# Two graph attention layers on one core: another order of the preparation, row blocks of features in pairs, and layer 1's groups ending without sums

## The chip, the core and the metric

The kernel runs on one core of one Trainium2 chip. The core has five engines with queues of their own: TensorE for matrix products and transposes (the profile shows its matmuls as PE and its weight loads as PEld), VectorE (DVE), ScalarE (ACT), GpSimd (POOL), and SyncE (SP), which here issues nearly all DMA transfers. Each queue is worked off in the order in which it was written; engines wait for each other through semaphores. The metric is device time in microseconds. The kernel before took 5032.46 us, the median of three runs (5031.23 to 5033.24).

## What is computed

Everything is float32. There are 4096 nodes with 512 features; `adj` is 4096 x 4096. Each layer normalises its input, clips it at zero and adds what an attention with 8 heads of 64 features makes of it:

```python
h = max(layernorm(x), 0)
# layer 0
d = h @ W.T + b                             # 4096 x (8 heads x 64)
e = src[:, None] + trg[None, :]             # for each head, from d
e = where(e >= 0, e, 0.01 * e) + adj
x = x + softmax(e) @ d
# layer 1
h = max(layernorm(x), 0)
a = (h Wq)(h Wk)^T / 8 - 1e16 * (1 - max(adj, eye))
x = x + sum over heads of softmax(a) @ (h Wv) @ Wo
```

The division by the sum of a softmax row can be made anywhere between its exponentials and `Wo`, since it is one factor for each row and head.

## The kernel before

A block is 128 rows (32 of them, `NB`). Heads go in pairs `c`; a **group** is one pair for one block. The program has five stretches.

**Preparation** (lines 419 to 446 call it). It takes the input in 8 turns `q` of four blocks. `load_rows` brings 1 MB of `x` into one of three buffers. `moments` has VectorE take means and variances (`bn_stats` at line 320, `bn_aggr` at 321) and ScalarE the root (line 323). `normed` inverts the root and has GpSimd write the normed rows `hn` (line 336). `turned_rows` transposes them on TensorE (`htp`, line 348), ScalarE clips them on the way out of PSUM (`hT`, line 351), and 1 MB of `hT` is stored (line 354). `halves` multiplies them with a small matrix that holds the source and target projections (`lp`, line 363); VectorE takes the result out as `lr` (line 368), and four small stores write the target halves to `trg_d` (line 370). After every second turn `load_targets` (line 128) loads 1024 columns of two heads' target halves back, spread over all partitions. `sources` transposes the source halves (`sp`, line 377), and `first_features` makes the first pair's features (`mp`, 32 matmul instructions at line 387, taken out by an add at line 393). The work of a turn is spread over five loop passes, so that pass `q` does the moments of turn `q`, the norm of `q - 1`, the transposes of `q - 2`, the halves of `q - 3`, and sources and features of `q - 4`. The tiles `htp`, `lp` and `mp` share three PSUM buffers.

**Layer 0, three pairs of heads** (lines 447 to 486): for each group ScalarE makes the logits (`leaky`, line 147), VectorE adds `adj` and takes the row extreme (`masked`, line 158), ScalarE takes exponentials (line 168), TensorE transposes (line 181) and multiplies with the features (line 203). `sources_by_sets` runs once, early in this stretch. **Layer 0's last pair together with layer 1's projections** follows (lines 735 to 780); the change doesn't touch it.

**Layer 1** (lines 1003 to 1060) has 512 sets, each 32 rows of a pair; four sets are a group, 128 groups in all. One pass `s` of the loop does, in this order on the queues: transposes of set `s - 4` on VectorE (line 936) and TensorE (line 942), the row extreme of an earlier pair of sets (`smallest`, `nmB`, line 913), one step of an ended group (`finish`), the scores of set `s` (line 878) and their masking by VectorE (line 894), the exponentials of set `s - 3` on ScalarE (line 929), and the product of set `s - 8` with the values (line 959). The mask comes from `adj` in pair 0 (GpSimd writes it at line 865) and from DRAM afterwards. `finish` copies the group's result out of PSUM (`oT`, line 969), adds the four sets' sums on TensorE (`den`, line 972), inverts them on VectorE (line 976), transposes the result in the next pass (`back`, line 979), multiplies (line 981) and stores 64 KB to `att_d` (line 985), which is laid out by rows.

**Output** (lines 1063 to 1084) starts when the loop is over: `wot` is loaded, then for each of 32 blocks `xt` and `at` are loaded, `at` is transposed (`atr`, line 1075), copied by ScalarE (line 1077), multiplied with `wot` (`oo`, 8 matmul instructions, line 1080), added (line 1083) and stored.

Of the kernel before, what the change touches and what calls it, by code (L numbers as in the profile page):

```python
# [15 lines left out]
P = 128  # L16
# [7 lines left out]
def kernel(  # L24
# [74 lines left out]
    with tc.tile_pool(name="a0k", bufs=1) as pk, tc.tile_pool(name="a0v", bufs=4) as pv, tc.tile_pool(  # L99
# [216 lines left out]
        def moments(R):  # L316
            R.mv = psb.tile([P, XR, 2], F32, name="mv")
            for r in range(XR):
                stats = psb.tile([P, 6], F32, name="stats")
                nc.vector.bn_stats(stats, R.x[:, r])  # L320
                nc.vector.bn_aggr(R.mv[:, r], stats)
            R.rstd = psb.tile([P, XR, 1], F32, name="rstd")
# [17 lines left out]
        def turned_rows(R, q):  # L340
# [3 lines left out]
            for j in range(XR // 2):  # L344
# [9 lines left out]
            nc.sync.dma_start(  # L354
                hT_d[bass.ts(q, XR)].rearrange("r p k -> p r k"), R.hT.rearrange("p r k n -> p r (k n)")
            )
# [25 lines left out]
        def first_features(R, q):  # L382

            tp = ptr.tile([P, TW], F32, tag="tr", name="mp")
            for r in range(XR):
                for kc in range(KC):
                    nc.tensor.matmul(
                        tp[:, bass.ts(r, PR)], lhsT=R.hT[:, r, kc, :], rhs=wt[:, kc, :PR],
                        start=(kc == 0), stop=(kc == KC - 1),
                    )  # L390
            if q % 2 == 0:
                feats[0].append(pv.tile([P, 2 * XR, PR], F32, tag="v", name="v"))
            nc.vector.tensor_add(
                feats[0][-1][:, bass.ts(q % 2, XR), :], tp[:, : XR * PR].rearrange("p (r d) -> p r d", r=XR),
                bb[:, :PR].unsqueeze(1).to_broadcast([P, XR, PR]),
            )

# [21 lines left out]
        with tc.manual_schedule():  # L419
# [6 lines left out]
            for q in range(NQ + 5):  # L426
                if q + 2 < NQ:
                    rows.append(load_rows(q + 2))
                if q < NQ:
                    moments(rows[q])  # L430
                if 0 <= q - 1 < NQ:
                    normed(rows[q - 1])
# [3 lines left out]
                if 0 <= q - 2 < NQ:  # L436
                    turned_rows(rows[q - 2], q - 2)
# [6 lines left out]
                if 0 <= n - 1 < NQ:  # L444
                    sources(rows[n - 1], n - 1)
                    first_features(rows[n - 1], n - 1)
# [4 lines left out]
            for s in range(total + 6):  # L451
                G, h = step(s) if s < total else (None, 0)
                for half in range(2):
# [8 lines left out]
                    if (s, half) == (1, 0):  # L462
# [9 lines left out]
                    if s < total:  # L472
                        masked(G, h, half)
                    for e in endings:
# [307 lines left out]
    att_d = dram.tile([N, HD], F32, name="att_d")  # L782
    pen_d = dram.tile([N // 32, P, N // 4], F32, name="pen_d")

# [9 lines left out]
    NT = (QK_ - VC) // P  # L794
    with tc.tile_pool(name="a1t", bufs=1) as pt, tc.tile_pool(name="a1k", bufs=4) as pkk, tc.tile_pool(
        name="a1v", bufs=GS
    ) as pv, tc.tile_pool(name="a1a", bufs=6) as pa, tc.tile_pool(name="a1q", bufs=2) as pq, tc.tile_pool(
        name="a1x", bufs=1
    ) as px, tc.tile_pool(name="a1s", bufs=6) as psb, tc.tile_pool(
# [313 lines left out]
```

## Time and profile before

| what | value |
|---|---|
| median of the runs | 5032.46 us |
| the profiled execution's own time | 5033.3 us, with a span of 5031.5 us |
| mean granted TensorE clock | 0.978 |
| busy, PE / DVE / ACT / POOL | 4802.4 / 4530.7 / 3929.0 / 362.1 us |
| weight loads, PEld | 3552.2 us |
| first `masked` of layer 0 starts | 110.62 us |
| scores of layer 1 from which the chain holds hardly anything but TensorE | 2588.67 us |
| last scores of layer 1 start | 4861.42 us |
| first transposes of the output | 4893.63 us |
| last matmul of the output ends | 5027.69 us |

The span is the time from the first to the last instruction of one profiled execution. A busy time is the sum of an engine's instruction times; matmuls overlap, so that a fully busy PE is not yet PE at its best. In the chain of waits each piece is the time until the next link could start, and "xN" counts instructions, two for each float32 matmul. A releaser is the event after which an idle engine went on.

### The profile page before, as it was taken

The page shows a single profiled execution, that of the slowest core. Times are in us where ns is not written, and L with a number is a line of the kernel's source. Part 1 is how long each engine was busy: PE and PEld are TensorE (multiplying, and loading weights), DVE is VectorE, ACT ScalarE, POOL GpSimd, SP SyncE. Part 2 cuts the span into 40 slices and gives each one's busy share as a digit, 9 for nine tenths or more (in the row PEclk, how much of TensorE's full clock was granted, in tenths as well). Part 3 has the DMA queues.
Part 4 walks back from the last instruction along what each step waited for, and adds up shares of the span by engine and source line. Part 5 has one row for each costly group of instructions (what it writes and reads, how often), then busy time and mean ns, then how long its engine had stood idle before and what let it go on. Part 6 is the DMA issues. An engine that isn't in the chain of part 4 may idle for free.

```text
span 5031.5 us, 147684 instructions
## 1 busy us (share of the span) xinstructions
PE 4802.4 (95%) x62810; PEld 3552.2 (71%) x62810; DVE 4530.7 (90%) x8205; ACT 3929.0 (78%) x4581; POOL 362.1 (7%) x648
## 2 busy tenths in 40 slices
PE   6999999999999869999989999999999999999999
PEld 5888888888888757677746666666666666666654
DVE  4999999999999898888579999999999999999971
ACT  3999999999999898888568888666666666666651
POOL 1000000000000011111112222000000000000000
PEclk8999999999999979999999999999999999999999
DMA  6444454445444474444387777433353434444425
GB/s 217 152 163 146 163 194 163 147 161 195 163 147 161 129 167 134 141 140 138 98 240 240 237 239 246 145 124 126 126 160 122 127 127 143 141 127 127 127 98 176
DMA packets 339908, 794.35 MB, mean 158 GB/s; under 512 B 57520, under 2 KB 168368, under 8 KB 314160
## 3 DMA queue, kind: packets, MB, share of 16 engines
q1 hardware_dynamic: 338720, 783.86, 48.7%
q8 instruction: 493, 8.08, 0.7%
q14 instruction: 167, 1.37, 0.1%
q10 hardware_dynamic: 528, 1.05, 0.1%
HBM read 652.48 MB, written 132.25 MB: 156 GB/s over the span
## 4 chain that ended last, share of the span: by engine, by line
PE 46%; DMA 1%; ACT 1%; issue 1%; DVE 1%; SPq 0%; POOL 0%; ACTq 0%; DVEq 0%; POOLq 0%
PE o L959 18%; PE sc L878 18%; PE tr L942 6%; PE oo L1080 2%; DMA a<-in_adj_dram 1%; ACT t L929 1%; PE nmB L913 1%; PE den L972 0%; DVE t L936 0%; PE back L979 0%; SPq L852 0%; PE mp L697 0%; DVE t L894 0%; ACT aT L1077 0%; PE mpv L709 0%
## 5 line engine op out<-in xcount | busy, mean ns | idle before, releaser
L894 DVE CUSTOM_DVE_ANT_0 t<-sc,a 128x512 f32<-128x512 f32 x2048 | 1291.1, 686 | 78.2 <-issue 56.3
L929 ACT ACTIVATE t<-t,nm 128x1024 f32<-128x1024 f32 x1024 | 1168.4, 1143 | 167.6 <-DVE nm L918 167.6
L959 PEld LDWEIGHTS o<-t,v 128*64 128x64 f32 x16384 | 883.9, 137 | 423.2 <-issue 339.7
L878 PE MATMUL sc<-k,q 64*32 64x512 f32 x16384 | 1002.5, 597 | 8.9 <-DVE nm L894 8.9
L959 PE MATMUL o<-t,v 128*64 128x128 f32 x16384 | 1007.0, 276 | 0.2 <-ACT oT L969 0.2
L936 DVE STREAM_TRANSPOSE t<-t 128x1536 f32<-128x1536 f32 x512 | 908.1, 1774 | 8.9 <-ACT t L929 5.9
L158 DVE CUSTOM_DVE_ANT_0 t<-t,a 128x2048 f32<-128x2048 f32 x384 | 876.1, 2282 | 28.7 <-ACT t L147 23.6
L181 PE MATMUL tr<-ident,t 128*128 128x128 f32 x6144 | 781.7, 278 | 38.1 <-ACT pT L190 20.0
L181 PEld LDWEIGHTS tr<-ident,t 128*128 128x128 f32 x6144 | 665.4, 141 | 130.6 <-issue 65.5
L203 PE MATMUL o<-pT,v 128*64 128x128 f32 x12288 | 756.8, 276 | 0.8 <-DVE pT L192 0.8
L147 ACT ACTIVATE t<-tb,src 128x4096 f32<-128x4096 f32 x192 | 732.0, 3813 | 13.7 <-DMA tb<-trg_d 13.7
L168 ACT ACTIVATE t<-t,nm 128x4096 f32<-128x4096 f32 x192 | 731.7, 3811 | 6.9 <-DVE nm L163 6.6
L203 PEld LDWEIGHTS o<-pT,v 128*64 128x64 f32 x12288 | 664.1, 137 | 60.7 <-issue 46.9
L948 ACT COPY t<-tr 128x512 f32<-128x512 f32 x512 | 298.9, 584 | 480.2 <-PE tr L942 477.4
L192 DVE COPY pT<-tr 128x1024 f32<-128x1024 f32 x549 | 652.7, 1214 | 9.8 <-PE tr L181 9.8
L878 PEld LDWEIGHTS sc<-k,q 64*32 64x32 f32 x16384 | 251.0, 106 | 340.7 <-issue 298.5
L942 PE MATMUL tr<-ident,t 128*128 128x128 f32 x2048 | 342.6, 287 | 11.5 <-ACT t L929 9.5
L569 ACT ACTIVATE lk<-tb,srcb 128x1024 f32<-128x1024 f32 x256 | 282.3, 1113 | 83.5 <-DVE nm L579 76.4
L579 DVE CUSTOM_DVE_ANT_0 bt<-lk,ba 128x1024 f32<-128x1024 f32 x256 | 301.9, 1215 | 25.6 <-ACT e L703 12.7
L618 DVE STREAM_TRANSPOSE bt<-bt 128x2048 f32<-128x2048 f32 x128 | 295.1, 2306 | 29.0 <-ACT bt L611 29.0
L942 PEld LDWEIGHTS tr<-ident,t 128*128 128x128 f32 x2048 | 213.7, 140 | 111.3 <-issue 85.0
L611 ACT ACTIVATE bt<-bt,nm 128x1024 f32<-128x1024 f32 x256 | 290.3, 1135 | 0.4 <-DVE nm L600 0.3
(116 smaller groups left out, 3961.4 us busy)
## 6 DMA issues: line engine op xcount, KB each, us to landing
a<-in_adj_dram SPq DMA_DIRECT2D x192, 1024.0 KB
a<-pen_d SPq DMA_DIRECT2D x384, 512.0 KB
ba<-in_adj_dram SPq DMA_DIRECT2D x512, 128.0 KB
a<-in_adj_dram SPq DMA_DIRECT2D x512, 128.0 KB
pen_d<-a SPq DMA_DIRECT2D x128, 512.0 KB
h<-hT_d SPq DMA_DIRECT2D x96, 256.0 KB
qk_d<-e SPq DMA_DIRECT2D x64, 256.0 KB
x<-in_x_dram SPq DMA_DIRECT2D x8, 1024.0 KB
```

Source lines behind the costliest of these rows:

```text
L147: nc.scalar.activation(t, targets[G.c, h], AF.Prelu, bias=src[:, G.g, 2 * G.c + h : 2 * G.c + h + 1], alpha=SLOPE)
L158: nc.vector.tensor_tensor_reduce(out=t, in0=t, in1=rows_of_adj[G, f], scale=-1.0, scalar=FMAX, op0=ALU.add, op1=ALU.min, accum_out=nm[:, f ...
L168: nc.scalar.activation(G.t[h], G.t[h], AF.Exp, bias=G.nm[h][:, NCH : NCH + 1], scale=-1.0, accum_out=G.sm[:, h : h + 1],)
L181: nc.tensor.transpose(tr[:, bass.ts(b % 4 * 2 + h, P)], G.t[h][:, bass.ts(i * MB + b, P)], ident)
L192: nc.vector.tensor_copy(pT, tr)
L203: nc.tensor.matmul(G.o[h * D : (h + 1) * D, :P], lhsT=feats[G.c][i][:, b, bass.ts(h, D)], rhs=pT[:, bass.ts(b % 4 * 2 + h, P)], start=(mb ...
L878: nc.tensor.matmul(sc[h][bass.ts(a, SQ), :], lhsT=G.q[bass.ts(h, D), bass.ds(G.q0 + k * SQ, SQ)], rhs=keys[G.c][half][bass.ts(h, D), a, :] ...
L894: nc.vector.tensor_tensor_reduce(out=t[:, G.ring + k, h, cols], in0=scs[half][h], in1=a[:, cols], scale=1.0, scalar=FMAX, op0=ALU.add, op1 ...
L929: nc.scalar.activation(u, u, AF.Exp, bias=G.nm[k // 2][:, k % 2, h : h + 1], scale=-1.0, accum_out=G.sm[:, k, h : h + 1],)
L936: nc.vector.transpose(u, u)
L942: nc.tensor.transpose(tr[:, bass.ts(h * NT + m, P)], t[:, G.ring + k, h, bass.ds(VC + m * P, P)], ident)
L959: nc.tensor.matmul(G.o[bass.ts(h, D), :P], lhsT=v[:, b, bass.ts(h, D)], rhs=t[:, bass.ds(G.ring, GS), h, bass.ds(at, SQ)], start=(mb == 0) ...
```

## The change

It has three parts.

1. **Preparation.** The root is split off `moments` as `deviations` and written after the transposes' copies of an earlier turn; transposes and norm stand ahead of the moments in a pass. Features are made for two blocks a pass instead of four (`first_features(q, j)`, 16 matmul instructions), their add is written at the start of the next pass (`first_features_out`), and the store of `hT` goes after a turn's second add. What is not made when the passes end (7 of 16 halves) is made in the first two sets of passes of layer 0's first group, beside its first logits. `sources_by_sets` moves from `(1, 0)` to `(3, 1)`.
2. **Layer 1's groups.** `finish` only copies the result out and stores it, still transposed and not divided, to `att_d`, which is now laid out by pair. The sums of all sets stay in one tile, `sums`. Once 16 groups of a pair are done, `divided` adds the sums with one matmul (`tot`), inverts, transposes (`invT`), writes the factors to `inv_d`, loads four pieces of `att_d` with their factors, multiplies them (GpSimd; VectorE for the last half) and stores them back.
3. **Output.** It runs inside layer 1's loop in the passes after the last scores (`projected`, one block a pass, ten in all), and after it for the other 22 blocks, from chunks of two blocks (`load_chunk`). `at` comes transposed already, so no transposes and no copies are left. The ninth chunk's load first runs whatever is left of the divisions.

```diff
-            for q in range(NQ + 5):
+            for q in range(NQ + 4):
                 if q + 2 < NQ:
                     rows.append(load_rows(q + 2))
+                some_out()
+                if 0 <= q - 2 < NQ:
+                    turned_rows(rows[q - 2], q - 2)
+                if 0 <= q - 1 < NQ:
+                    normed(rows[q - 1])
                 if q < NQ:
                     moments(rows[q])
-                if 0 <= q - 1 < NQ:
-                    normed(rows[q - 1])
+                    deviations(rows[q])
                 if q == 1:
                     prepared(wn, col)
                     turned_weights(wn)
-                if 0 <= q - 2 < NQ:
-                    turned_rows(rows[q - 2], q - 2)
...
                 if 0 <= n - 1 < NQ:
                     sources(rows[n - 1], n - 1)
-                    first_features(rows[n - 1], n - 1)
+                some_features(q - 2)
+            some_out()
...
+                    if s < 3:
+                        some_features(NQ)
+                        some_features(NQ)
...
         def finish(G):
             oT = px.tile([P, P], F32, name="oT")
             nc.scalar.copy(oT, G.o[:, :P])
-            den = pm.tile([P, 512], F32, tag="ms", name="den")
...
+            nc.sync.dma_start(att_d[G.c, :, bass.ts(G.g, P)], oT)
+
+        def inverted(c, half):
+            tot = pm.tile([P, 512], F32, tag="ms", name="tot")
+            nc.tensor.matmul(
+                tot[:, : 2 * SG * GS], lhsT=bands,
+                rhs=sums[:, c, half].rearrange("p h g k -> p (h g k)"), start=True, stop=True,
+            )
+            inv = px.tile([P, P], F32, tag="oT", name="inv")
+            nc.vector.reciprocal(inv[:SQ], tot[:SQ, : 2 * SG * GS])
+            yield
+            invT = pm.tile([P, 512], F32, tag="ms", name="invT")
+            nc.tensor.transpose(invT[:, :SQ], inv[:SQ], ident[:SQ, :SQ])
+            rows = px.tile([P, SQ], F32, name="rows")
+            nc.scalar.copy(rows, invT[:, :SQ])
+            for h in range(2):
+                nc.sync.dma_start(
+                    inv_d[c, h, bass.ts(half, SG * P)].rearrange("(q i) -> q i", i=SQ), rows[bass.ts(h, D)]
+                )
+            yield
+
+        def scaled(c, half):
+            last = (c, half) == (HC - 1, 1)
+            zs = []
+            for i in range(4):
+                cols = bass.ts(half * 4 + i, 4 * P)
+                z = pz.tile([P, 2, 4 * P], F32, tag="z", name="z")
+                nc.sync.dma_start(z[:, 0], att_d[c, :, cols])
+                for h in range(2):
+                    nc.sync.dma_start(z[bass.ts(h, D), 1], inv_d[c, h, cols].partition_broadcast(D))
+                yield
+                zs.append((cols, z))
+                if i % 2 == 0:
+                    continue
+                yield
+                for cols, z in zs:
+                    (nc.vector if last else nc.gpsimd).tensor_mul(z[:, 0], z[:, 0], z[:, 1])
+                yield
+                for cols, z in zs:
+                    nc.sync.dma_start(att_d[c, :, cols], z[:, 0])
+                zs = []
...
+        def load_chunk():
+            i = len(chunks)
+            if i >= NG // 2 // ZR:
+                for d in divisions:
+                    for _ in d:
+                        pass
+                divisions.clear()
+            if i < NB // ZR:
+                at = pat.tile([P, HC, ZR * P], F32, name="at")
+                nc.sync.dma_start(at, att_d[:, :, bass.ts(i, ZR * P)].rearrange("c p n -> p c n"))
+                xt = pa.tile([P, ZR, DM], F32, tag="a", name="xt")
+                nc.sync.dma_start(xt, x1_d[bass.ts(i, ZR * P), :].rearrange("(r p) d -> p r d", p=P))
+                chunks.append((at, xt))
+
+        def projected(j):
...
+            nc.vector.tensor_add(xt[:, r], xt[:, r], o)
+            if r == ZR - 1:
+                nc.sync.dma_start(out[bass.ts(i, ZR * P), :].rearrange("(r p) d -> p r d", p=P), xt)
+                load_chunk()
...
+                if n > 1 and n % (SG * GS) == 1:
+                    divisions.append(divided(*divmod(n // (SG * GS) - 1, 2)))
+                for d in divisions[:1]:
+                    if next(d, d) is d:
+                        divisions.pop(0)
...
-        for rb in range(NB):
-            xt = pw.tile([P, DM], F32, name="xt")
...
+            for j in range(rb, NB):
+                projected(j)
```

## The prediction

> **What bounds the kernel now.** I first read the busy time by stretch (columns: stretch; total; busy time and instructions of PE, PEld, DVE, ACT, POOL; granted clock; DMA share; GB/s), because the 95% that the page gives PE is an average over stretches with different limits.
>
> ```profile
> 50.00:100.00 50.00, 43.20 (x469) 40.47 (x468) 16.93 (x50) 10.24 (x13) 12.06 (x16) 0.89 0.65 227
> 2900.00:2950.00 50.00, 49.77 (x792) 30.75 (x784) 49.31 (x122) 41.40 (x67) 11.76 (x16) 1.00 0.75 242
> 3300.00:4000.00 700.00, 700.00 (x11056) 437.84 (x11062) 670.86 (x1551) 461.63 (x815) 18.66 (x78) 1.00 0.42 132
> 4900.00:4950.00 50.00, 49.66 (x150) 24.08 (x149) 8.25 (x12) 6.44 (x12) 0.00 (x0) 0.99 0.58 185
> ```
>
> Preparation (first row) has no full engine, so a loop of waits bounds it. In layer 1 (second row pair 0, third row later pairs) TensorE is full, with VectorE close behind: 98.6% in pair 0, 95.8% later. In the output (last row) TensorE works alone. The timeline of one preparation turn (start, length, what, idle before and its releaser) shows the loop:
>
> ```profile
> 61.80 0.69 DVE L393 TENSOR_TENSOR v<-mp,bb 128x512 f32<-128x512 f32 x1 [6.11 <-PE mp L387]
> ...
> 65.60 0.14 DVE L326 RECIPROCAL rstd<-rstd 128x4 f32<-128x4 f32 x1
> 65.78 0.30 ACT L323 ACTIVATE rstd<-mv,eps 128x4 f32<-128x4 f32 x1 [8.63 <-DVE rstd L326]
> ...
> 65.99 1.92 ACT L351 ACTIVATE hT<-htp 128x1024 f32<-128x1024 f32 x2
> ...
> 67.04 5.46 PE L387 MATMUL mp<-wt,hT 128*128 128x128 f32 x32 [2.27 <-ACT hT L351]
> ```
>
> The add waits for the features; behind it VectorE's moments wait; ScalarE's root waits for them and its copies `hT` stand behind the root; the features wait for a PSUM buffer that the copies free. Once round is 10.75 us (this add at 61.80, the next at 72.55). The chain of waits (start, length, link) gives one group of layer 1, then the output:
>
> ```profile
> 4757.56 0.17 PE den L972 x8
> 4757.73 1.88 PE sc L878 x32
> 4759.61 1.90 PE o L959 x32
> 4761.50 0.59 PE tr L942 x4
> 4762.09 0.14 PE nmB L913 x2
> 4762.23 0.14 PE back L979
> ...
> 4887.35 6.14 DMA at<-att_d
> ...
> 4895.39 6.29 PE oo L1080 x8
> ...
> 4999.10 0.59 ACT aT L1077
> 4999.69 0.04 issue
> 4999.73 7.13 PE oo L1080 x16
> ```
>
> In the group every link is TensorE, end to end: taking one out moves everything up. In the output two blocks take 7.13 us of matmuls out of 8.08 (4999.73 to 5007.82); the rest is transposes and the copy.
>
> **Preparation: -19 us.** The new order cuts the loop: the copies `hT` no longer stand behind the root, the add no longer waits for matmuls written just before it. What a pass then costs each engine, by the durations of the old loop: PE `htp` 1.91, `lp` 1.08, `sp` 0.33, half the features 1.9 to 2.7 (32 took 3.74 to 5.46), some 0.5 of issue gaps: about 6.0 us. DVE four times 0.66 + 0.18, plus 0.30 for root and shift, 0.35 `lr`, 0.18 `src`, an estimated 0.4 for half an add: 4.6. ACT 2.2, POOL 3.0. So TensorE bounds, at 6.0. The first logit halves start at 34.15 now and about 34.5 after (the start, up to 30 us, is the same small matrix products and copies). Six turns of 6.0, the last pass shorter, put the eighth at about 73.5; it starts at 96.27 now. That is 22.8 saved, and the first `masked` at 110.62 hangs on it by the same steps (target stores, their reload, `leaky`, `adj`). Against it: on SP's queue the fourth `hT` store now stands between the last reload and the first `adj` tile, 1 MB more to move, 2.6 us at the 400 GB/s that DMA reaches at best here. Three more `hT` stores stand ahead of the fourth `adj` tile, which waits for VectorE anyway and is needed some 16 us later. The seven late feature halves fill a TensorE that idles there (its first long run of transposes starts at 128.00), so they are free; without that cover they cost 7 x 1.9. Their adds are 7 x 0.4 = 2.8 on VectorE, part of it inside its waits for ScalarE (2.6 and 1.95 us there): 1.2. The moved `sources_by_sets` made VectorE wait 1.38 before and may again: nothing. Ends: -27 (warm clock, 5.5 a pass, nothing given back) and -10 (a pass moves 2 MB; at 290 GB/s that is 7.2 us, not 6.0).
>
> **Layer 1: -35 us.** `den` and `back` leave the chain: 0.17 + 0.14 = 0.31 a group; 125 of the 128 groups end before the tail begins: 38.8. VectorE loses 0.275 + 0.131 a group; of an 18.04 us group it is busy 17.29 in later pairs, so 16.88 against TensorE's new 17.73, and in pair 0 17.8 - 0.4 = 17.4. TensorE stays the bound; in pair 0 with 0.3 to spare. The result copy stays on ScalarE, and the store behind it on SP stands ahead of a mask load that is five sets early. What is added: seven divisions inside the loop. `tot` and `invT` are not in the trace; by the nearest rows (`nmB` 0.14 for two matmuls, a transpose 0.15) about 0.3. The inverse on VectorE waits for `tot`, which stands behind TensorE's last product of that pass, and the next `squares` wait behind the inverse: up to 0.5 late. I take 0.6 in all, 4.2 for seven; ends 0.3 and 1.7. The transfers of a division (3 MB over some ten passes) have room at 132 GB/s.
>
> The 28 multiplications on GpSimd have no row of their own. Two-input rows there are 240 ns for 32 columns and 458 for 128; carried on to 512 columns that is an estimated 1.34 us, two in a row. Behind them waits only the next `parted`, needed two sets later. One rule speaks against this: the Trainium skill, *GPSIMD Engine Reference*, Key points, says that GpSimd shares its SBUF interfaces with VectorE, so that the two get in each other's way when VectorE runs a two-port mode or reads two SBUF tensors. If a pair held VectorE up for its whole 2.7 us, the slack of 0.85 a group would hide a third, and 14 pairs would cost about 26 us. The rows say otherwise: with GpSimd busy 11.76 of 50 us in pair 0, line 894 took 683 ns, and 687 in later pairs without it; line 936 took 1778 and 1773. GpSimd's work there has one input, so the two-input case is not quite shown. I take nothing, and 13 for the range.
>
> **Output: -17 us.** From 4865.20, where the last regular transposes start, the span runs 166.3 us. After: TensorE has 8 x 1.90 of products, 4 x 0.59 of transposes and 0.14: 17.7; 32 blocks of 3.57 (7.13 / 2): 114.2; 0.4 for the last division. The ten interleaved blocks fill the waits for ScalarE that this tail has now, so these add up end to end: 132.3. Behind the last matmul, as now, an add and a store: 3.8, and 0.7 for a store twice as large. That would be 136.8, 29.5 less than now.
>
> But the ninth chunk waits for the last half's division, and that is a chain through DRAM. It is started from SP only behind the store of block 11: add and store issue, 1.1. Then: load two pieces with factors (1 MB in six issues; the reload of 1 MB of targets took 4.3 from issue at 102.00 to `leaky` at 106.29: 5.0 with four issues more), two multiplications on VectorE at 0.69 (line 1083), store (the last one took 3.1 to the end of the span), load again 5.0 because there are two buffers, multiply 1.4, store 3.1, load chunk 4.0: 24.1 in all. TensorE has blocks 12 to 15 meanwhile, 14.3 (four PSUM buffers, so no add holds them up). So it stands still for about 10, and starts again at a low clock: eight instructions took 6.29 after the 6 us wait of now, 3.57 otherwise, 2.7 more. 29.5 - 12.7 = 17. Ends: -29 (the chain is covered) and -5 (each of the loads takes the 6.14 us of the output's first one and the chunk behind queues too).
>
> **Sum.** -19 - 35 - 17 = -71 from the span of 5031.5: 4960.5. The profiled execution reported 5033.3 and the median of the runs is 5032.46, 1 us above the span, so 4962.
>
> **Rivals.** *No stall in the output* (0.17): the division's transfers are short enough or start early enough. For it: 256 KB pieces with DMA engines 58% busy; against it: five steps, each waiting for the one before. 4949. *Preparation bounded by transfers or SP* (0.12): 2 MB a pass, and SP's reloads wait for the small stores to land (10.2 us in six waits now, the longest 5.8). It gives -8 instead of -19: 4973. *VectorE takes over in layer 1* (0.10): pair 0 is at 98.6% and GpSimd's pairs collide: half the gain is lost, 4980. *Slower than before* (0.03): the division chain costs far more. Its place is the ninth chunk, its price per step; without it the change is worth 84, so it decides from 84 + 14.3 for five DMA steps, about 20 us a step. The longest single wait for a load in the output is 6.14 us, so I hardly believe it; at 22 us a step it would be 5044. That the change doesn't do what it says I exclude: with the order of instructions at hand, `den`, `back` and `atr` are gone.
>
> **How the numbers follow.** The forecast case has 0.55, its own range 4948 to 4976. The range 4942 to 4985 takes in all but the slower case and the far ends of the unknown costs. A change under 0.2% (10 us) can't be told from none here. All cases but the last are over it: faster 0.95, same 0.02, slower 0.03.
>
> **What would show it.** Preparation: adds of features 6 us apart instead of 10.75, first logits near 80 instead of 106.29. Layer 1: group period 17.73 instead of 18.04, lines for `tot` eight times, line 894's mean still near 687 in windows with multiplications. Output: no transposes, one hole of 10 us in TensorE at block 16, fed by a DMA. I am wrong if adds stay 8 us or more apart, if VectorE's idle in layer 1 vanishes, or if the hole is missing or longer than 20.

## The result, and the profile after

The changed kernel takes 4974.47 us (median of 4 runs, 4972.49 to 4976.71), beside 5032.85 us (5031.23 to 5037.03) for the kernel before in the same comparison. The ratio is 0.9883, with a 95% interval of 0.9866 to 0.9900. The profiled span went from 5031.5 to 4973.0 us, so 58.5 us are to be found, where the prediction had 71.

Where they came from can be read by the starts of the same instructions in both traces. VectorE's 32x32 transposes of layer 1 (`squares`) are good marks: four a group, 512 in all.

| stretch, by its marks | before | after | change | predicted |
|---|---|---|---|---|
| start to the first `squares` of layer 1 | 2566.30 | 2551.35 | -14.9 | -19 |
| pair 0, first two groups | 35.25 | 37.69 | +2.4 | -0.6 |
| pair 0, the other 30 groups | 548.76 | 547.22 | -1.5 | -8.7 |
| pairs 1 to 3, 95 groups | 1714.74 | 1688.71 | -26.0 | -25.9 |
| from there to the end of the span | 166.45 | 148.03 | -18.4 | -17 |

The last column splits the prediction's -35 for layer 1: 0.31 us a group, less 0.6 for each division, one of them in pair 0 and six later. The rows of pairs 1 to 3 and of the end are right within 1.5 us. The misses are pair 0 (both of its rows) and, less so, the preparation.

The busy time by stretch of the changed kernel (columns: stretch; total; busy time and instructions of PE, PEld, DVE, ACT, POOL; granted clock; DMA share; GB/s):

```profile
50.00:100.00 50.00, 30.64 (x321) 28.38 (x320) 13.21 (x33) 14.24 (x10) 6.03 (x8) 0.80 0.74 260
2900.00:2950.00 50.00, 49.66 (x760) 30.30 (x744) 49.04 (x115) 42.49 (x70) 15.35 (x20) 1.00 0.91 288
3300.00:4000.00 700.00, 699.97 (x10888) 437.25 (x10889) 673.08 (x1499) 468.04 (x830) 28.90 (x87) 1.00 0.43 143
4880.00:4930.00 50.00, 40.01 (x87) 17.36 (x86) 9.45 (x15) 0.00 (x0) 0.00 (x0) 0.86 0.71 229
```

In the second row, pair 0, VectorE is still busy for 49.04 of 50 us (before 49.31), although two of its operations a group are gone. A busy share that hardly falls when work is removed is the sign to look there. The last row shows a hole in TensorE in the output, 10 us in 50, and a granted clock of 0.86 with it.

A group of a later pair in the chain of waits (start, length, link) is the old one without `den` and `back`:

```profile
4741.61 1.88 PE sc L915 x32
4743.49 1.90 PE o L996 x32
4745.39 0.58 PE tr L979 x4
4745.97 1.88 PE sc L915 x32
...
4759.20 0.14 PE nmB L950 x2
4759.34 1.88 PE sc L915 x32
```

From 4741.61 to 4759.34 are 17.73 us, the predicted period; before it was 18.05. The output's end in the same view:

```profile
4889.30 4.70 DMA z<-inv_d
...
4894.12 0.70 DVE z L1044
...
4894.85 1.99 DMA att_d<-z
...
4899.59 4.12 DMA z<-inv_d
...
4904.93 5.34 DMA at<-att_d
...
4910.40 58.01 PE oo L1079 x128
```

The last half's division runs through DRAM link by link and hands over to TensorE at 4910.40, 23.7 us after the products of block 11 ended (4886.69), which the last store ahead of it waited for.

The timeline of VectorE in the preparation (start, length, what, idle before and its releaser):

```profile
45.06 0.42 DVE L396 TENSOR_TENSOR v<-mp,bb 128x256 f32<-128x256 f32 x1
...
49.42 0.42 DVE L396 TENSOR_TENSOR v<-mp,bb 128x256 f32<-128x256 f32 x1
...
55.92 0.69 DVE L320 BATCH_NORM_STATS2 stats<-x 128x6 f32<-128x512 f32 x1 [5.79 <-DMA x<-in_x_dram]
...
59.67 0.42 DVE L396 TENSOR_TENSOR v<-mp,bb 128x256 f32<-128x256 f32 x1
```

The adds come 4.4 to 5.3 us apart here (35.34, 39.81, 45.06 and 49.42: 4.7 on the mean), better than the 6 predicted, and then once 10.25 us apart: VectorE waits for the last rows.

### The profile page after: what moved, and what is told of

Same layout as the page of the kernel before. It is cut to its first block, busy times and chain, and to the rows that moved or that the text cites. A ratio compares the mean times of both kernels' runs of the same rounds, so it can differ in the third digit from the quotient of the medians.

```text
span 4973.0 us, 145263 instructions
## 1 busy us (share of the span) xinstructions
PE 4747.3 (95%) x61554; PEld 3507.7 (71%) x61554; DVE 4509.1 (91%) x7969; ACT 3912.2 (79%) x4557; POOL 396.1 (8%) x676
## 4 chain that ended last, share of the span: by engine, by line
PE 42%; DMA 3%; issue 2%; SPq 1%; ACT 1%; DVE 1%; POOL 0%; ACTq 0%; POOLq 0%; DVEq 0%
PE sc L915 17%; PE o L996 17%; PE tr L979 5%; PE oo L1079 2%; DMA a<-in_adj_dram 2%; ACT t L966 1%; PE nmB L950 1%; SPq L889 1%; POOL a L902 0%; DVE t L931 0%; PE mp L727 0%; DMA z<-inv_d 0%; PE mpv L739 0%; DMA att_d<-z 0%; DMA v<-v_d 0%
## 5 line engine op out<-in xcount | busy, mean ns | idle before, releaser
L973 DVE STREAM_TRANSPOSE t<-t 128x1536 f32<-128x1536 f32 x512 | 907.7, 1773 | 5.0 <-ACT t L966 2.0
L979 PE MATMUL tr<-ident,t 128*128 128x128 f32 x2048 | 348.5, 288 | 11.6 <-ACT t L966 8.4
```

What stands on the lines that cost most here:

```text
L973: nc.vector.transpose(u, u)
L979: nc.tensor.transpose(tr[:, bass.ts(h * NT + m, P)], t[:, G.ring + k, h, bass.ds(VC + m * P, P)], ident)
```

## The experiments

The runs were timed in other comparisons than the result, in which the kernel before had medians of 5032.50 to 5033.90. Differences of two or three us between medians are no more than this spread; where a gain is that small, the marks of the profiled runs carry the reading.

### Pair 0: what holds 18.3 us a group

The periods of single groups, from start to start of every fourth `squares`, were steady in pair 0: 18.35 us before and 18.31 after (medians over 22 groups). The prediction had used 18.04 for both. The timeline of all engines of the changed kernel shows one set of four (weight loads, reads of accumulators and the small operations left out):

```profile
2970.24 1.15 ACT L966 ACTIVATE t<-t,nm 128x1024 f32<-128x1024 f32 x1 [1.26 <-DVE nm L955]
...
2972.52 1.04 ACT L901 ACTIVATE a<-a 128x1024 f32<-128x1024 f32 x1
...
2972.89 1.78 DVE L973 STREAM_TRANSPOSE t<-t 128x1536 f32<-128x1536 f32 x1
...
2973.64 1.04 POOL L902 TENSOR_SCALAR a<-a 128x1024 f32<-128x1024 f32 x1 [4.41 <-ACT a L901]
...
2974.72 0.69 DVE L931 CUSTOM_DVE_ANT_0 t<-sc,a 128x512 f32<-128x512 f32 x1
```

The masked logits start 1.83 us after `squares`, 0.04 us after GpSimd's mask is done (2973.64 + 1.04). Where nothing is waited for, a following operation starts 1.70 us after. The mask depends on ScalarE's relu, which stands behind ScalarE's exponentials, which wait for VectorE's minimum (the first line): a loop of some 18.3 us a group. The theory made from this: before, VectorE's own work filled the period and the mask lay just under it; the change took instructions of 0.41 us out of that work, and the mask's wait took their place. Four runs test it.

**Masks two sets ahead, in the changed kernel:**

```diff
+            with_self(*step(1), pens[1])
+            made_penalty(*step(1), pens[1])
...
-                if s + 1 < total:
-                    with_self(*step(s + 1), pens[s + 1])
+                if s + 2 < total:
+                    with_self(*step(s + 2), pens[s + 2])
...
-                if s + 1 < total:
-                    made_penalty(*step(s + 1), pens[s + 1])
+                if s + 2 < total:
+                    made_penalty(*step(s + 2), pens[s + 2])
```

> The changed kernel, with pair 0's mask tiles made two sets ahead instead of one (the diagonal on VectorE, the relu on ScalarE and the scaling on GpSimd all one set earlier); nothing is left out. Theory 1 (the mask chain took up what the change freed): in pair 0 VectorE's own work is now 18.0 us a group (two times 4.45 + 4.55), the other 0.32 is the wait of the plain sets for GpSimd's tile; it goes, the period falls from 18.32 to 18.0 and 32 groups give 10 us: about 4964. Rival (VectorE is simply full at 18.3, its busy share is 98%): the period stays at 18.3 and the time at 4974. Rival 2 (TensorE would have bound at 17.73 but for the mask): 32 x 0.59 = 19 us, 4955.

Measured: 4972.68 us (4972.26 to 4976.67), by its range not to be told from the changed kernel; the profiled span is 1.9 less. The period is what the theory said, and the time isn't. The median group takes 18.00 us, and the wait is gone:

```profile
2966.03 1.78 DVE L973 STREAM_TRANSPOSE t<-t 128x1536 f32<-128x1536 f32 x1
...
2966.77 1.05 POOL L902 TENSOR_SCALAR a<-a 128x1024 f32<-128x1024 f32 x1 [4.10 <-DMA a<-in_adj_dram]
...
2967.73 0.65 DVE L931 CUSTOM_DVE_ANT_0 t<-sc,a 128x512 f32<-128x512 f32 x1
```

1.70 us from `squares` to masked logits. (The mask beside them is that of a later set.) Over the last 30 groups of pair 0 this gives 5.1 us (547.22 to 542.12) and not 9: one group at a division rose to 20.36 us, because the mask now needs its adj tile a set sooner and SP issues that tile behind the division's loads. And 5 us are lost where layer 1 begins, since two masks must be made before the first logits: the first `squares` come 3.6 us later, and the first eight sets take 1.3 us more. So the wait is shown, and with it the cost of an edit that moves work of a start-up.

**The same edit in the kernel before:**

> The kernel before, with the same edit: pair 0's masks made two sets ahead. Theory 1 (before, VectorE's own work of 4.45 + 4.55 + 4.60 + 4.75 = 18.35 us a group set the period, and the mask chain lay just under it): no gain, 5032 within 3, period 18.35. Rival (the mask chain set the period of pair 0 before as well): 10 us faster, 5022, period 18.0.

Measured: 5035.26 us against 5033.39, ratio 1.0002 (0.9993 to 1.0011). The median period fell by 0.09 us, from 18.35 to 18.26, against 0.31 in the changed kernel. So before, the mask was close behind but VectorE's own work set the pace, as the theory has it. The rows of both runs without the mask's wait (this run, then the changed kernel's) show how a full VectorE looks here: 98.6% busy, the rest in gaps too short to have a releaser.

```profile
2750.00:2850.00 100.00, 100.00 (x1564) 61.51 (x1562) 98.61 (x242) 84.27 (x139) 25.44 (x33) 1.00 0.74 237
```

```profile
2750.00:2850.00 100.00, 100.00 (x1539) 61.49 (x1545) 98.55 (x235) 85.33 (x140) 25.81 (x34) 1.00 0.74 238
```

Between these two runs the change is worth 18.26 - 18.00 = 0.26 us a group, not 0.41, although the two instructions that it removed lasted 0.41.

**The diagonal off VectorE as well.** GpSimd multiplies the finished corner of the mask by one minus the identity:

```diff
-                nc.vector.tensor_max(diag, diag, ident[bass.ts(b, SQ), bass.ts(b, SQ)])
+                nc.gpsimd.tensor_mul(diag, diag, other[bass.ts(b, SQ), bass.ts(b, SQ)])
...
                 nc.gpsimd.tensor_scalar(a, a, -1.0, -BIG, ALU.add, ALU.mult)
+                with_self(G, k, a)
```

> The changed kernel with the masks two sets ahead and the diagonal taken from VectorE (0.18 us and some 0.03 beside it, four times a group): GpSimd multiplies the finished 32x32 corner by one minus the identity. Same result, nothing left out. Theory 1: VectorE's work in pair 0 falls to about 17.2 us a group, TensorE's 17.73 becomes the bound there too: 32 x 0.59 = 19 us under the changed kernel, about 4955, period 17.7 to 17.8. Rival (GpSimd's two-input work beside VectorE's two-input work slows VectorE, or the longer mask chain binds again): period 18.0 or more, 4964 or more.

One part of the computation is changed here, other than the expectation says: adj holds weights up to 1e9 and not only zeros and ones, and a node's own edge loses its weight. The instructions are those intended. Measured: 4963.05 us (4961.15 to 4966.00), median period 17.73 us, and for the 30 groups 534.35 us, 12.9 less than the changed kernel. The period is the theory's, the time 8 us more: the first `squares` come 4.0 us sooner, but the first eight sets take 44.8 us instead of 37.7. TensorE fills the stretch, and VectorE has room for the first time:

```profile
2800.00:2900.00 100.00, 99.98 (x1553) 62.62 (x1557) 96.21 (x213) 86.77 (x141) 34.67 (x58) 1.00 0.75 240
```

The rival's slowdown isn't there. The groups of VectorE and GpSimd in 200 us of pair 0 (busy, mean ns; idle before):

```profile
L934 DVE CUSTOM_DVE_ANT_0 t<-sc,a 128x512 f32<-128x512 f32 x180 | 113.5, 686 | 7.2 <-issue 3.9 <-POOL a L899 0.2 <-POOL a L904 0.2
L899 POOL TENSOR_TENSOR a<-a,other 32x32 f32<-32x32 f32 x45 | 11.0, 245 | 3.8
L1047 POOL TENSOR_TENSOR z<-z 128x512 f32<-128x512 f32 x2 | 2.5, 1290 | 0.1
```

GpSimd now runs a two-input operation in each set, and VectorE's masked logits, which take `sc` from PSUM and only the mask from SBUF, still take 686 ns.

**The diagonal as a sum ahead of the relu,** with only the first mask made before the loop:

```diff
-                nc.vector.tensor_max(diag, diag, ident[bass.ts(b, SQ), bass.ts(b, SQ)])
+                nc.gpsimd.tensor_add(diag, diag, ident[bass.ts(b, SQ), bass.ts(b, SQ)])
...
-                nc.scalar.activation(a, a, AF.Relu)
-                nc.gpsimd.tensor_scalar(a, a, -1.0, -BIG, ALU.add, ALU.mult)
+                nc.scalar.activation(a, a, AF.Relu, bias=one, scale=-1.0)
+                nc.gpsimd.tensor_scalar(a, a, BIG, None, ALU.mult)
```

> The changed kernel with pair 0's masks two sets ahead from the second set on, and the diagonal added on GpSimd (a 32x32 sum) ahead of ScalarE, which takes relu(1 - a); GpSimd then scales. The masks are the same for this matrix of zeros and ones. Theory 1 (VectorE's 0.21 us a set and the mask chain were all that stood between pair 0 and TensorE's 17.73 us): steady groups of 17.73 us instead of 18.30, about 24 of them, 12 to 14 us under the changed kernel, 4961. Rival (GpSimd and VectorE get in each other's way on two-input work): the masked logits rise above 0.70 us each and the groups stay at 18.0 or more, 4967 or more.

The expectation is mistaken about the matrix, for the reason above: this form drops the weights of all edges above one. Measured: 4967.91 us (4965.36 to 4969.21). The first groups take 17.73 us, the later ones 17.87 (median), and two at a division 20.17 and 20.36. The period is no longer VectorE's: ScalarE's relu now waits for GpSimd's sum (25.2 us in 200), and the sum stands on GpSimd's queue behind the scaling of another set, which has become slow. As a product with one constant it takes 2.77 us a tile; as a sum and a product with two constants it took 1.05. Why the simpler form is the slower one is not shown. So the time is the rival's, but not its reason: the masked logits still take 0.69 us.

```profile
L904 POOL TENSOR_SCALAR a<-a 128x1024 f32<-128x1024 f32 x44 | 121.9, 2771 | 56.0 <-ACT a L903 43.3 <-DMA a<-in_adj_dram 10.2 <-ACT rows L1023 1.3
```

### The output: is the division the hole?

The last half of the last pair is no longer divided through DRAM. A chunk loads its undivided columns and the inverses, and VectorE multiplies one chunk ahead:

```diff
+                zi = None
+                if i >= NG // 2 // ZR:
+                    zi = pat.tile([P, ZR * P], F32, name="zi")
+                    for h in range(2):
+                        nc.sync.dma_start(
+                            zi[bass.ts(h, D)], inv_d[HC - 1, h, bass.ts(i, ZR * P)].partition_broadcast(D)
+                        )
...
             if r == ZR - 1:
+                if i + 1 < len(chunks) and chunks[i + 1][2] is not None:
+                    nat, _, nzi = chunks[i + 1]
+                    nc.vector.tensor_mul(nat[:, HC - 1], nat[:, HC - 1], nzi)
```

> The changed kernel, in which the last half of the last pair is not divided through DRAM: each of the last eight output chunks loads its undivided columns and the inverses beside them, and VectorE multiplies (0.35 us a chunk) one chunk ahead. Same result, nothing left out. Theory 1: the stores, loads and multiplications of the division are the 23.6 us chain that leaves TensorE idle for some 10 us at block 16; the hole goes, with the 1 us of its cold restart: 4964, one unbroken run of output products. Rival (the hole is that of loads queued late behind the outputs' stores, not of the division): a hole of 4 us or more stays at block 16 and the gain is under 6 us. Rival 2 (VectorE's multiplications hold up the adds and so the buffers): gain under 6 us, with several small holes.

Measured: 4962.83 us (4960.20 to 4964.17), 11.6 less than the changed kernel; the profiled span is 12.9 less. The chain of waits has no hole left:

```profile
4875.95 0.22 PE tot L1011 x2
4876.17 3.44 PE oo L1086 x8
4879.61 0.17 PE invT L1019
4879.78 75.75 PE oo L1086 x176
```

22 blocks in 75.75 us are 3.44 each. In the changed kernel the 16 blocks after the hole took 58.01, so 3.63 each. The difference, 16 x 0.183 = 2.9 us, is the restart at a low clock (0.50 from 4910.4 to 4916.1, 1.00 from there on); the other 10.0 are the hole. Both rivals are out.

### The preparation: why not all of it

**The preparation alone, in the kernel before** (layer 0 of the changed kernel, layer 1 and the output of the kernel before):

> The kernel before with the changed preparation alone; layer 1 and the output stay as before. Theory 1 (the parts of the change add up, and the first products of layer 1 come 15.8 us sooner in the changed kernel because of the preparation alone): 5033 - 15.8 = 5017, first scores of layer 1 near 2527. Rival (the preparation's gain is partly lost again in layer 1, whose start stands cold in the changed kernel): 5020 or more.

Measured: 5020.32 us against 5032.50 (ratio 0.9973, 0.9962 to 0.9983); the profiled span fell by 14.4. The first `squares` come at 2551.50, 14.8 sooner. The median is the rival's, by little (5020 or more). The first eight sets of layer 1 take 36.4 us instead of 35.2: a part of the gain is lost again there, with the old code of layer 1. The changed kernel loses 2.4 there. Yet two kernels with its code in layer 1 (late reloads, and small stores moved, both below) take 35.4 and 35.2, so the change in layer 1 alone is not the cause either.

What decides can be read by comparing the changed kernel with the one with late reloads. TensorE's wait where layer 1 begins is as long in both (7.50 and 7.52 us), and so is the clock for the next 18 us. Then a few hundredths of a us decide. In the changed kernel VectorE's maximum on the diagonal comes 0.05 us after GpSimd's scaling has started, and ends only when the scaling does:

```profile
2564.54 1.04 POOL L902 TENSOR_SCALAR a<-a 128x1024 f32<-128x1024 f32 x1 [2.45 <-ACT a L901]
...
2564.59 1.02 DVE L897 TENSOR_TENSOR a<-a,ident 32x32 f32<-32x32 f32 x1
...
2568.70 0.44 PE L979 MATMUL tr<-ident,t 128*128 128x128 f32 x2 [2.28 <-ACT t L966]
```

With late reloads it comes 0.04 us ahead of the scaling and takes 0.17:

```profile
2563.32 0.17 DVE L903 TENSOR_TENSOR a<-a,ident 32x32 f32<-32x32 f32 x1
...
2563.36 1.05 POOL L908 TENSOR_SCALAR a<-a 128x1024 f32<-128x1024 f32 x1 [2.44 <-ACT a L907]
...
2566.59 0.44 PE L985 MATMUL tr<-ident,t 128*128 128x128 f32 x2 [1.35 <-ACT t L972]
```

So TensorE's next wait is 2.28 us instead of 1.35, and the granted clock of the 12 us from the fifth set on is 0.86 instead of 1.00. The kernels in which a maximum was held up in the first 16 us took 37.6 us or more for the eight sets, those without 35.2 to 36.4. This is read from the traces; no run changes it alone, and with the preparation alone 1.1 us went although no maximum was held up before the clock fell.

**Reloads one pass later.** SP issued the load of the last rows behind a reload of targets, which waits for stores:

```diff
             for q in range(NQ + 4):
                 if q + 2 < NQ:
                     rows.append(load_rows(q + 2))
+                if 0 <= q - 4 < NQ - 1:
+                    reload_targets(q - 4)
...
-                    if (n + 1) * XR % TB == 0:
-                        for h in range(2):
-                            load_targets(0, h, n * XR // TB, NB // TB)
+                    if n == NQ - 1:
+                        reload_targets(n)
```

> The changed kernel, in which the reloads of the first three quarters of the targets stand one pass later in SP's queue, behind the load of the next rows instead of ahead of it. Theory 1 (VectorE's 5.8 us wait for the last rows comes from SP standing at the reload, which waits for the target stores to land): the rows' load is issued some 4 us sooner, the wait falls under 2 us, TensorE keeps its clock, the first logits come 4 to 5 us sooner: 4970. Rival (the wait is one for bandwidth: 2 MB a pass): the wait stays above 4 us, 4974. Rival 2 (the gain at the rows is lost again at the last reloads): first logits as before, 4974.

Measured: 4971.87 us (4970.55 to 4975.24), 2.6 less. VectorE's wait for the last rows falls from 5.79 us to 0.47:

```profile
51.67 0.69 DVE L320 BATCH_NORM_STATS2 stats<-x 128x6 f32<-128x512 f32 x1 [0.47 <-DMA x<-in_x_dram]
```

The eighth `lr` comes at 66.81 instead of 72.63, 5.8 us sooner. But the last reload is issued at 80.21 instead of 82.35, and the first leaky logits come only 2.1 us sooner. The stall was as the theory has it; most of its price was paid a second time, at SP's next jam. That is rival 2. At the first `squares` 1.2 us are left; another 2.3 are those of the first eight sets.

**Stores of hT from ScalarE's queue:**

> The changed kernel, in which the eight stores of hT are issued from ScalarE's queue instead of SP's. Theory 1 (SP's small stores wait 8.3 us for hT stores to land, and the last reload is issued 9.7 us after the eighth block of logit halves because of it): the last reload is issued 3 to 5 us sooner, the first adj tiles come sooner too, the first masked logits 5 to 8 us: about 4968. Rival (the waits come from the transfers themselves, whatever queue they stand in): less than 2 us, 4973. Rival 2 (ScalarE, standing at a store, is late with copies and logits): slower, 4976 or more.

Measured: 4973.09 us (4970.84 to 4973.37), 1.4 less, not to be told from none by the medians. The last reload stands 9.0 us behind the eighth `lr`, hardly less than 9.7, so it is not the place of the hT stores in SP's queue that holds it. (By the profile the small stores still wait 5.2 us there for an hT store to land, 6.0 in the changed kernel.) The first masked logits come 2.7 us sooner; the first adj tile no longer stands behind an hT store.

**Both:**

> Both edits of the preparation together. Theory 1 (two different stalls of SP, one in mid-preparation, one at its end): their gains add, about 10 us under the changed kernel, 4964. Rival (one stall shifted about): no more than the better of the two.

Measured: 4970.82 us (4970.19 to 4972.90), 3.7 less. The first masked logits come at 87.96, 5.8 sooner, and at the last ones of layer 0's main loop the lead is still 5.6. At the first `squares` of layer 1 it is 3.9. The single leads of 2.0 and 2.7 add, and a little more, but they are smaller than expected.

**The small target stores from ScalarE's queue**, together with the late reloads. SP's queue at the end of the preparation, in the changed kernel:

```profile
71.51 0.82 SPq L128 DMA_DIRECT2D tb<-trg_d  x2
72.37 0.43 SPq L402 DMA_DIRECT2D hT_d<-hT  x1
72.84 8.41 SPq L369 DMA_DIRECT2D trg_d<-lr  x8
82.35 0.82 SPq L128 DMA_DIRECT2D tb<-trg_d  x2
```

Eight stores of 4 KB hold the queue for 8.41 us, though the last of their data were there at 72.98 (`lr` at 72.63, 0.35 long), and the last reload stands behind them. The time passes between the issues, where the profile shows waits for other transfers to land:

```profile
SPq L369 <- DMA hT_d<-hT: 6.0, 2, 3.7
```

```diff
-                nc.sync.dma_start(
+                nc.scalar.dma_start(
                     trg_d[:, bass.ts(q * XR + r, P)], R.lr[r * SQ + H : r * SQ + 2 * H, :]
                 )
```

> The changed kernel with the first three quarters of the targets reloaded one pass later (as in the run before) and with the small target stores issued from ScalarE's queue instead of SP's; hT stays on SP. Theory 1 (the end of the preparation is SP's queue: small stores, 4 KB each, issued one behind another's landing, stand ahead of the last reload): the last reload is issued within 5 us of the eighth logit halves instead of 13.4, first leaky logits 7 to 9 us sooner than in the changed kernel, 4966. Rival (the small stores themselves take long to land, whatever the queue): the reload stays 9 us or more behind, first leaky logits 2 us sooner as with the late reload alone, 4972.

Measured: 4966.83 us (4964.26 to 4967.87), 7.6 less than the changed kernel. The last reload is issued at 74.97, 7.0 us behind the eighth `lr` instead of 13.4 with the late reload alone (the theory had 5), and the first leaky logits come at 78.93, 7.4 sooner:

```profile
78.93 7.31 ACT L147 ACTIVATE t<-tb,src 128x4096 f32<-128x4096 f32 x2 [13.30 <-DMA tb<-trg_d]
```

So SP's order bounded the end of the preparation. The stores themselves remain slow (eight took 7.94 us on ScalarE's queue too, where the last four had their data at 68.30 and were issued by 72.98), which is the part of the rival that holds. Of the gain, 5.3 us stand at the first `squares`; 2.4 more come from the first eight sets, which took 35.2 us here.

### Together

**Four of these edits** (masks as in the sum ahead of the relu, scaling in the chunks, late reloads, hT on ScalarE's queue):

> The changed kernel with four edits together: masks two sets ahead with the diagonal on GpSimd, the last half scaled in its chunks, late reloads, hT stores from ScalarE's queue. Theory (the places are independent): the sum of the single gains under the changed kernel, 12 (output) + 12 (masks) + 4 (preparation) = 28, about 4946. Rival (what is gained in the preparation is absorbed where layer 1 starts, as with the two preparation edits, where 5.6 us at the end of layer 0 became under 4): 4949.

Measured: 4950.10 us (4948.52 to 4953.89); the edge weights are dropped as above. The single gains 11.6, 6.6 and 3.7 make 21.9, and 24.4 were measured: the places add up. The theory's 28 had counted on a single gain of 12 from the masks.

**The best of each.** The diagonal's maximum becomes minus the identity on GpSimd, relu, plus the identity; adj tiles are loaded six sets ahead, the small stores leave SP:

```diff
-                nc.vector.tensor_max(diag, diag, ident[bass.ts(b, SQ), bass.ts(b, SQ)])
+                op = nc.gpsimd.tensor_add if back else nc.gpsimd.tensor_sub
+                op(diag, diag, ident[bass.ts(b, SQ), bass.ts(b, SQ)])
...
                 nc.scalar.activation(a, a, AF.Relu)
+                with_self(G, k, a, back=True)
                 nc.gpsimd.tensor_scalar(a, a, -1.0, -BIG, ALU.add, ALU.mult)
...
-            AHEAD = 5
+            AHEAD = 6
```

> The changed kernel with what the runs so far point to, together: masks two sets ahead; the diagonal's maximum taken from VectorE, as minus the identity on GpSimd, relu on ScalarE, plus the identity on GpSimd; adj tiles loaded six sets ahead with a seventh buffer; the last half scaled in its chunks; late reloads and the small target stores on ScalarE's queue. It computes what the changed kernel computes, but for rounding. Theory (three independent places): under the changed kernel's 4974.5, the output gives 11.6, the preparation 7.6, pair 0 some 24 x 0.45 = 11 and its two division stalls of 2.5 us: about 4942. Rival (the adj tiles of pair 0 still come late behind the divisions' loads in SP's queue): groups above 20 us stay at the divisions, 4947 to 4950.

Measured: 4947.14 us (4943.12 to 4949.15), ratio to the kernel before 0.9827 (0.9813 to 0.9840), 27.3 us under the changed kernel. The time is the rival's, but not for its reason. The groups at the division of pair 0 take at most 19.27 us, the steady ones 17.73, and the row of pair 0 shows VectorE and TensorE as wanted:

```profile
2800.00:2900.00 100.00, 99.99 (x1554) 62.92 (x1552) 96.21 (x217) 87.30 (x141) 38.53 (x79) 1.00 0.75 236
```

By the marks of the profiled run against the changed kernel: 11.8 us sooner at the first `squares`, 7.3 lost in the first eight sets (44.96 instead of 37.69), 13.1 won in the other 30 groups, 12.3 in the output. The first two must be read together, since moving the masks moves work between them: with masks ahead and the diagonal on GpSimd alone they are 4.0 won and 7.1 lost, with the small stores moved 5.3 and 2.4 won. These sums, -3.1 and 7.7, make the 4.5 found here. So the start of layer 1 costs some 3 us for the earlier masks.

## Why the prediction was right, and where it wasn't

*Output, -17, measured -18.4: right, and for its reason.* The chain was worked out as 24.1 us and took 23.7; the hole "about 10" is 10.0 by the run without it, the restart of 2.7 is 2.9. The rival without a stall is out. The blocks were a little shorter than the 3.57 taken (3.44 without the hole).

*Pairs 1 to 3: right.* 0.32 us a group over 95 groups are 30.1. A division costs its group 1.02 us and the next one gives 0.34 back, so 0.68 net against 0.6. GpSimd's multiplication takes 1.29 us (estimated 1.34), and masked logits and `squares` stay at 686 and 1773 ns over the whole run. So taking nothing for it was right, but not for the reason given. The rule of the Trainium skill, *GPSIMD Engine Reference*, Key points, that the prediction weighed speaks of VectorE reading two SBUF tensors. The rows that were held against it don't: the masked logits read one operand from PSUM, and `squares` has one input. Where VectorE does read two, in the maximum on the diagonal of pair 0, this case's traces agree with the page. It takes 0.18 us alone; started just after GpSimd's scaling, it ends with it:

```profile
2871.25 1.04 POOL L902 TENSOR_SCALAR a<-a 128x1024 f32<-128x1024 f32 x1 [4.25 <-DMA a<-in_adj_dram]
...
2871.27 1.06 DVE L897 TENSOR_TENSOR a<-a,ident 32x32 f32<-32x32 f32 x1
```

With masks two sets ahead a multiplication of the division held it as well (0.50 us). The estimate of 26 us could not come true in the later pairs, where VectorE reads no two SBUF tensors. In pair 0 the hold-up is 0.88 of the 1.70 us by which the group at the division is longer (20.00 and 18.30).

*Pair 0: the step that failed.* The prediction wrote "in pair 0 17.8 - 0.4 = 17.4. TensorE stays the bound; in pair 0 with 0.3 to spare". Two things were wrong in this step. It multiplied pair 0's busy share by the period of the later pairs; pair 0's own was 18.35 us. And it took the idle 1.4% as spare: 98.6% of 18.35 less 0.41 would still have been 17.7, just under TensorE's 17.73. The runs with the masks ahead show that 98.6% is VectorE full. After the change its pace is 18.00 us, and the wait for the mask, for which there was no term, fills it up to 18.31. So the 30 groups gave 1.5 us instead of 8.7. Two runs show the two layers: 18.00 without the mask's wait, 17.73 with the diagonal off VectorE too. The rival "VectorE takes over in layer 1" was right for this pair and had the wrong size and reach: VectorE did not take over there, it had bound already.

*Start of layer 1: no term for it.* 2.4 us were lost in its first two groups, with a lower granted clock, where a few hundredths of a us put VectorE's maximum behind GpSimd's scaling. With the preparation alone 1.1 us were lost.

*Preparation, -19, measured -14.9: right in kind, with one term badly mis-sized.* The eighth `lp` came at 71.42, where 73.5 was forecast: passes of 4.7 us instead of 6.0 paid for the wait of 5.79 us for the last rows, and left 2. What failed is "by the same steps". From the eighth `lp` to the first leaky logits it took 10.0 us before and 15.0 after (86.37, forecast near 80), because the last reload stood 9.7 us behind the eighth `lr`, where before it was 4.5. From there to the first masked logits it took 3.0 us more than before, where 2.6 was taken for the `hT` store, and 1.9 more went by the first `squares` of layer 1, where 1.2 was taken for the late adds. The prediction counted the hT store behind the last reload but not the small stores ahead of it, on the same queue. It had them as a rival, "bounded by transfers or SP": that was right of the queue, and too dark with -8.

The total fell inside the range because the sum's large terms held, and the errors of pair 0, of layer 1's start and of the preparation all went one way: 7.2 + 3.0 + 4.1, less the 1.4 won in the output. That is 13 us less gain than forecast, and 4974.47 lies just inside the 4976 that ended the forecast case's own range.

## What to carry to other kernels

Take a stage's period from that stage, by start-to-start times of one instruction, before multiplying a busy share by it. When work is taken from an engine that is full, ask what waits just under it: here a loop through three engines lay just under VectorE's own work, and instructions of 0.41 us, worth 0.26 without that loop, bought 0.04. An engine can be full below 100%: read how busy it is where nothing but its own work holds it. Where a loop of compute is shortened, read the issuing queue of its transfers next: small stores and the reload that waits for them hold everything queued behind them, and moving them to another queue, besides the later reload, brought the first `squares` 5.3 us sooner, where moving the large ones brought 3.9.

## What the runs showed of the hardware

- The issue of small stores is slow when others are under way: eight of 4 KB took SP 8.41 us and ScalarE's queue 7.94, while the 1 MB store of `hT` between them took 0.43.
- VectorE's maximum with both inputs in SBUF (32x32, 0.18 us alone) took up to 1.06 us where an operation of GpSimd had started first: over the ten kernels that have it, it then ended 0.03 to 0.04 us after GpSimd's in 22 of 24 cases, and in the other two GpSimd's was nearly over. Started first, it kept its 0.18.
- VectorE's masked logits, with one operand in PSUM and one in SBUF, stayed at 686 ns beside GpSimd's sums and products with two inputs.
- GpSimd's scaling of 128x1024 took 2.77 us as a product with one constant and 1.05 as a sum and a product with two.
- After the output's hole the clock was 0.50 for 5.7 us, and cost 2.9 us over 16 blocks of matmuls.
